# Moving a scale into the forget gates, and four 512-element operations to GpSimd, in a three-stage software pipeline

## The chip, the cores and the metric

The kernel runs on one core of a Trainium2 chip. A core has five engines that run side by side, each taking its own instructions strictly in order, and that wait for each other through semaphores: PE (TensorE, matrix products into PSUM), DVE (VectorE, elementwise), ACT (ScalarE, functions from tables), POOL (GpSimd, [...] the issuing of some DMAs) and SP (SyncE, the other DMAs). The metric is the device time of one execution in microseconds (us). Before the change it is 5087.27 us, the median of three runs (5086.96 to 5087.37).

## The reference, cut to what matters

The program is four layers on an image of 256x256 pixels with 128 channels. Layer 1 is the one touched here; its 128 channels are the real and imaginary parts of 64 complex ones. A complex spectrum A is taken from a 7x7 kernel, scaled to a bounded magnitude, and applied 16 times per pixel with a gate for each part:

```python
mag = jnp.sqrt(Ar ** 2 + Ai ** 2 + 1e-08)
scale = 0.95 * jax.nn.sigmoid(mag) / (mag + 1e-08)
Ar = Ar * scale
Ai = Ai * scale
...
def step(h_state, _):
    h_r, h_i = h_state
    Ah_r = Ar * h_r - Ai * h_i
    Ah_i = Ar * h_i + Ai * h_r
    return ((fg_r * Ah_r + inp_r, fg_i * Ah_i + inp_i), None)
```

The 16 steps multiply by the same 2x2 matrix per pixel and channel, M = [[fr Ar, -fr Ai], [fi Ai, fi Ar]]. The kernel therefore doesn't loop over the steps: with the trace t = (fr + fi) Ar and the determinant d = fr fi (Ar² + Ai²) it forms the sum of the first 16 powers of M as a polynomial by repeated squaring (squares of t and d, 2nd, 4th, 8th, 16th).

## The kernel before, in words

`recurrence` handles the image in NB = 64 blocks of four image rows. A block is a set of tiles of 128 partitions by 512 elements (called thin) or by 2x512 = 1024 (called wide), all float32. The work of a block is cut into about 75 small steps, each a one-line function named after what it makes. One hand-written tuple, `order`, lists (step, lag) pairs: iteration `it` runs each step for block `it - lag`, so three blocks are in work at once. Every step is pinned, so that each engine's instruction order is the order of this tuple restricted to the engine. The steps that matter below:

- lag 0: the products `zd`, `za`, `zf` (PE); `zaa`, which copies the spectrum out of PSUM into `ar`, and `a2`, its square (ACT); `m2`, the sum of the two squares (PE); `lm`, `mg`, `lb`, `iv`, `sg`, the functions that give the magnitude and its inverse (ACT); `f`, the two forget gates (ACT); `q`, then `s`, the scale, then `A`, which multiplies `ar` by the scale (DVE).
- lag 1: `A2`, the square of the scaled A (ACT), and `pa`, the sum of its two halves (PE); `ff` and `pf`, product and sum of the gates, `d_` (which reads `pa`), `t`, `D_` (DVE); the squarings `tq2`, `tq4`, `tq8`, `tq16`, `dn2`, `dn4`, `dn8` (ACT) between `tr2`, `u2`, `tr4`, `u4`, `tr8`, `u8` (DVE); the input path `zb`, `zi`, `bx` (PE), `xn`, `ig` (ACT), `p0`, `p1`, `qg`, `v` (DVE); `xa`, `y1` (DVE).
- lag 2: `y0`, `tr16`, `xb`, `be`, `e_`, `al` (DVE); `av` (PE); `yf`, `t1`, `yb` (DVE); `pox`, `po1`, `po2` (PE); `ev_`, `bn` (ACT). `ev_` also starts the DMA that writes the block (POOL's queue, L1044).

In the profile the DVE steps appear as L914 (two-operand, through `tt`) and L917 (scalar-and-two-operand, through `stt`), ACT steps as L54, its table loads as L889, PE steps as L60; a step is recognised by its tiles: the numbers are left out of names, so `tq2` to `tq16` are all `tq`, `tr2` to `tr16` `tr`, `u2` to `u8` `u`, `y0` and `y1` `y`. `t<-u,t` is `al`, `t<-t,g` is `e_`, `g<-t,u` is `xa`, `q<-q,ig` is `qg`.

PSUM is full: the products of tag "z" (`zd`, `za`, `zb`, `zf`, `zi`) share two buffers, those of tag "y" (`bx`, `av`, `po`) share one, and those of tag "s" (`m2`, `pa`) two of one bank each. So `av` can't begin until `v` has read `bx`, `pox` not until `yf` has read `av`, and the next `bx` not until `ev_` has read `po`.

## Time and profile before

| what | us |
|---|---|
| median of three runs | 5087.27 |
| span of the profiled execution | 5083.0 |
| the recurrence, first `zd` to last `ev_` | 1697.0 to 3219 |
| its steady part, one iteration per 23.31 us | 1734 to 3179 |
| PE, DVE, ACT busy in those 1445.0 us | 1406.31, 1444.89, 1392.10 |
| POOL busy there (62 DMA issues) | 33.11 |

The profile holds one execution, and its time is its span, 5083.0 us from the first to the last instruction; the 4.3 us up to the median of the runs lie around the span. [...] back to back, DVE starts a 512-element operation every 0.60 us and a 1024-element one every 1.135 us, though one lasts 0.69 and 1.22. The 62 iterations from 1734 to 3179 repeat to a hundredth of a microsecond.

### The profile page before, as it was taken

The page shows a single profiled execution, that of the slowest core. Times are in us where ns is not written, and L with a number is a line of the kernel's source. Part 1 is how long each engine was busy: PE and PEld are TensorE (multiplying, and loading weights), DVE is VectorE, ACT ScalarE, POOL GpSimd, SP SyncE. Part 2 cuts the span into 40 slices and gives each one's busy share as a digit, 9 for nine tenths or more (in the row PEclk, how much of TensorE's full clock was granted, in tenths as well). Part 3 has the DMA queues.
Part 4 walks back from the last instruction along what each step waited for, and adds up shares of the span by engine and source line. Part 5 has one row for each costly group of instructions (what it writes and reads, how often), then busy time and mean ns, then how long its engine had stood idle before and what let it go on. Part 6 is the DMA issues. An engine that isn't in the chain of part 4 may idle for free.

```text
span 5083.0 us, 78992 instructions
## 1 busy us (share of the span) xinstructions
PE 4951.9 (97%) x31563; PEld 2715.8 (53%) x31563; DVE 4100.4 (81%) x4797; ACT 3496.8 (69%) x4948; POOL 406.9 (8%) x592
## 2 busy tenths in 40 slices
PE   8999999999999899999999999899999999999999
PEld 2444555555555333333333333329999953359999
DVE  6666999999999799999999999775333537779886
ACT  6445888888888899999999999453333357762110
POOL 0331000000000000000000000240111010000000
PEclk9999999999999999999999999999999999999999
DMA  8894222222222222222222221688667778865432
GB/s 290 292 338 173 88 80 84 84 80 88 84 80 84 68 68 68 72 64 76 64 73 67 72 68 60 218 324 309 237 229 243 252 286 321 324 233 180 142 122 67
DMA packets 204463, 781.69 MB, mean 154 GB/s; under 512 B 56278, under 2 KB 59628, under 8 KB 154788
## 3 DMA queue, kind: packets, MB, share of 16 engines
q1 hardware_dynamic: 146638, 505.57, 29.8%
q0 software_dynamic: 56160, 270.64, 14.8%
q8 instruction: 252, 4.13, 0.3%
q14 instruction: 117, 0.96, 0.1%
q10 hardware_dynamic: 1296, 0.40, 0.0%
HBM read 505.18 MB, written 271.32 MB: 153 GB/s over the span
## 4 chain that ended last, share of the span: by engine, by line
PE 57%; DVE 29%; issue 5%; ACT 1%; POOL 0%; DMA 0%; POOLq 0%; DVEq 0%; SPq 0%; ACTq 0%
PE z L60 9%; PE m L60 7%; PE nd L60 7%; PE sc L60 5%; PE zc L60 5%; PE po L60 4%; DVE tr L917 3%; DVE t L914 3%; DVE y L914 3%; DVE p L914 3%; DVE yf L914 3%; PE ppq L60 3%; PE ppv L60 2%; PE px L60 2%; PE pe L60 2%
## 5 line engine op out<-in xcount | busy, mean ns | idle before, releaser
L576 DVE TENSOR_TENSOR e<-sc,bT 128x1024 f32<-128x1024 f32 x512 | 603.1, 1220 | 49.8 <-PE sc L60 48.9
L54 ACT ACTIVATE e<-e 128x1024 f32<-128x1024 f32 x512 | 540.4, 1055 | 61.5 <-DVE e L576 52.4
L1077 DVE TENSOR_TENSOR LR<-z,sg 128x512 f32<-128x512 f32 x256 | 268.4, 1049 | 363.0 <-ACT sg L54 363.0
L60 PE MATMUL m<-U,v 128*128 128x128 f32 x4608 | 514.8, 275 | 0.0
L60 PEld LDWEIGHTS m<-U,v 128*128 128x128 f32 x4608 | 514.6, 192 | 0.0
L60 PE MATMUL z<-wf,zt 128*128 128x128 f32 x4096 | 459.6, 276 | 1.4 <-DVE zn L1077 1.4
L60 PEld LDWEIGHTS z<-wf,zt 128*128 128x128 f32 x4096 | 459.4, 192 | 2.3 <-DVE zn L1077 2.2
L54 ACT ACTIVATE sg<-z 128x512 f32<-128x512 f32 x256 | 152.9, 597 | 307.7 <-PE z L60 307.7
L54 ACT ACTIVATE sq<-zs 128x1024 f32<-128x1024 f32 x192 | 202.4, 1054 | 192.1 <-DVE zs L385 156.1
L576 DVE TENSOR_TENSOR ks<-e 128x1024 f32<-128x1024 f32 x256 | 301.0, 1217 | 0.0
L60 PE MATMUL sc<-tq,tk 32*128 32x256 f32 x4096 | 297.0, 401 | 3.0 <-DVE e L576 2.1
L60 PEld LDWEIGHTS sc<-tq,tk 32*128 32x128 f32 x4096 | 186.4, 184 | 159.6 <-issue 96.3
L60 PE MATMUL nd<-e,tv 128*32 128x256 f32 x4096 | 271.0, 382 | 0.0
L54 ACT ACTIVATE dn<-dn 128x512 f32<-128x512 f32 x384 | 241.9, 630 | 13.0 <-DVE dn L576 2.3
L60 PE MATMUL av<-y,ident 128*128 128x512 f32 x384 | 192.9, 611 | 44.0 <-DVE y L914 44.0
L60 PE MATMUL po<-LR 128*128 128x256 f32 x1024 | 222.2, 380 | 6.9 <-DVE LR L1077 6.9
L1462 ACT COPY m4s<-m 128x512 f32<-128x512 f32 x32 | 18.7, 583 | 287.2 <-PE m L60 287.2
L60 PEld LDWEIGHTS po<-LR 128*128 128x128 f32 x1024 | 194.1, 190 | 34.2 <-DVE LR L1077 7.7
L60 PE MATMUL bx<-p,ident 128*128 128x512 f32 x384 | 192.4, 610 | 0.0
L54 ACT ACTIVATE o<-po 128x256 f32<-128x256 f32 x256 | 84.3, 381 | 145.3 <-issue 110.5
L60 PEld LDWEIGHTS nd<-e,tv 128*32 128x32 f32 x4096 | 120.1, 109 | 108.2 <-issue 42.1
L889 ACT ACT_TABLE_LOAD x132 | 169.4, 1283 | 1.5
(366 smaller groups left out, 10321.1 us busy)
## 6 DMA issues: line engine op xcount, KB each, us to landing
zt<-znT SPq DMA_DIRECT2D x128, 1024.0 KB
znT<-zn POOLq DMA_DIRECT2D x64, 1024.0 KB, 5.2
xin<-x2T SPq DMA_DIRECT2D x64, 1024.0 KB
xin<-in_x_dram SPq DMA_DIRECT2D x50, 1024.0 KB
xr<-x3T SPq DMA_DIRECT2D x46, 768.0 KB
xT<-xo POOLq DMA_DIRECT2D x32, 1024.0 KB, 9.3
xr<-xT SPq DMA_DIRECT2D x64, 512.0 KB
zn<-znT SPq DMA_DIRECT2D x64, 512.0 KB
```

Of the source, the lines that this page charges most:

```text
L54: return self.nc.scalar.activation(out, in_, func, bias=bias, scale=scale, **kw)
L60: return self.nc.tensor.matmul(out, lhsT, rhs, start=start, stop=stop)
L576: pin = lambda f: lambda *a, **k: tc.keep_in_program_order(f(*a, **k))
L889: pin(nc.scalar.preload_act_table_set(want))
L914: pin(V.tensor_tensor(out, a, b_, op))
L917: pin(V.scalar_tensor_tensor(out, a, k, b_, op0, op1))
L1077: pin = lambda f: lambda *a, **k: tc.keep_in_program_order(f(*a, **k))
L1462: nc.scalar.copy(m4, m[4])
```

## The change

The scale is no longer multiplied into A. Since A only ever enters as f times A, the two forget gates are multiplied by it instead (`fs_` in place of `A`, of the same size), the determinant reads the unscaled `m2`, and `A2` and `pa` go. `ff`, `u2` and `al` go from DVE to GpSimd, `tq4` from ACT to GpSimd, and some entries of `order` are moved. The DMA of `ev_` is pinned into the same order. `ar` gets a second buffer, `A` and `A2` vanish.

```diff
+            def gt(out, a, b_, op):
+                pin(nc.gpsimd.tensor_tensor(out, a, b_, op))
...
-            def zaa(d): act(wide(d, "ar"), d["za"].rearrange("p r i v -> p i r v"), AF.Copy)
-            def A(d):
-                sb = d["s"].rearrange("p (r v) -> p r v", v=N).unsqueeze(2).to_broadcast([P, 2, 2, N])
-                tt(rows(wide(d, "A", 2)), rows(d["ar"]), sb, MUL)
-            def A2(d): act(wide(d, "A2"), d["A"], AF.Square)
-            def pa(d): total(d, "pa", [[(self.ident, d["A2"][:, 0]), (self.ident, d["A2"][:, 1])]])
-            def ff(d): tt(thin(d, "ff"), d["f"][:, 0], d["f"][:, 1], MUL)
+            def zaa(d): act(wide(d, "ar", 2), d["za"].rearrange("p r i v -> p i r v"), AF.Copy)
+            def fs_(d): tt(d["f"], d["f"], both(d["s"]), MUL)
+            def ff(d): gt(thin(d, "ff"), d["f"][:, 0], d["f"][:, 1], MUL)
...
-            def t(d): tt(thin(d, "t", 2), d["fs"], d["A"][:, 0], MUL)
-            def d_(d): tt(thin(d, "d", 2), d["pa"][:, 0], d["ff"], MUL)
+            def t(d): tt(thin(d, "t", 2), d["fs"], d["ar"][:, 0], MUL)
+            def d_(d): tt(thin(d, "d", 2), d["m2"][:, 0], d["ff"], MUL)
...
-            def u2(d): tt(thin(d, "u2"), d["t"], d["tr2"], MUL)
-            def tq4(d): squared(d, "tq4", "tr2")
+            def u2(d): gt(thin(d, "u2"), d["t"], d["tr2"], MUL)
+            def tq4(d): gt(thin(d, "tq4"), d["tr2"], d["tr2"], MUL)
...
-            def al(d): tt(d["t"], d["u8"], d["t"], SUB)
-
-            def y0(d): tt(wide(d, "y0"), d["A"], both(d["v"][:, 0]), MUL)
-            def y1(d): tt(wide(d, "y1"), d["A"], both(d["v"][:, 1]), MUL)
+            def al(d): gt(d["t"], d["u8"], d["t"], SUB)
+
+            def y0(d): tt(wide(d, "y0"), d["ar"], both(d["v"][:, 0]), MUL)
+            def y1(d): tt(wide(d, "y1"), d["ar"], both(d["v"][:, 1]), MUL)
...
-                nc.gpsimd.dma_start(x2T[:, b * 1024:(b + 1) * 1024], d["x2"])
+                pin(nc.gpsimd.dma_start(x2T[:, b * 1024:(b + 1) * 1024], d["x2"]))
...
-                (zd, 0), (y0, 2), (tr16, 2), (za, 0), (xn, 1), (ff, 1), (A2, 1), (ab, 0), (pa, 1), (av, 2), (ae, 0),
+                (zd, 0), (y0, 2), (tr16, 2), (za, 0), (xn, 1), (ab, 0), (av, 2), (ae, 0),
                 (xb, 2), (d_, 1), (eD, 2), (pf, 1), (a2, 0), (al_, 0), (be, 2), (zaa, 0), (dn2, 1), (t, 1), (dn4, 1),
-                (m2, 0), (e_, 2), (lm, 0), (yf, 2), (zb, 1), (al, 2), (D_, 1), (t1, 2), (yb, 2), (pox, 2), (tq2, 1),
-                (po1, 2), (po2, 2), (mg, 0), (tr2, 1), (lb, 0), (lD, 1), (zf, 0), (p0, 1), (p1, 1), (iv, 0), (u2, 1),
-                (sg, 0), (tq4, 1), (ev_, 2), (f, 0), (q, 0), (tr4, 1), (s, 0), (dn8, 1), (zi, 1), (u4, 1), (A, 0),
-                (bx, 1), (tq8, 1), (ig, 1), (tr8, 1), (qg, 1), (bn, 2), (u8, 1), (tq16, 1), (v, 1), (xa, 1), (y1, 1),
+                (m2, 0), (e_, 2), (lm, 0), (al, 2), (yf, 2), (zb, 1), (D_, 1), (t1, 2), (yb, 2), (pox, 2), (tq2, 1),
+                (po1, 2), (po2, 2), (mg, 0), (tr2, 1), (lb, 0), (lD, 1), (zf, 0), (u2, 1), (tq4, 1), (p0, 1), (p1, 1), (iv, 0),
+                (sg, 0), (ev_, 2), (f, 0), (q, 0), (tr4, 1), (s, 0), (dn8, 1), (zi, 1), (u4, 1), (fs_, 0),
+                (bx, 1), (tq8, 1), (ig, 1), (tr8, 1), (qg, 1), (bn, 2), (u8, 1), (tq16, 1), (v, 1), (ff, 0), (xa, 1), (y1, 1),
```

On GpSimd the order per iteration becomes `al`, `u2`, `tq4`, the DMA of `ev_`, `ff`. On DVE it is that of before without `ff`, `u2` and `al`, with `fs_` where `A` was.

## The prediction

> **What bounds the kernel now.** I read the table of stages first, for the steady part of the recurrence alone (columns: stretch, its length, then busy time and instructions of PE, PEld, DVE, ACT, POOL, the clock, DMA share, GB/s):

> ```profile
> 1734.00:3179.00 1445.00, 1406.31 (x4713) 468.00 (x4712) 1444.89 (x1798) 1392.10 (x2047) 33.11 (x62) 1.00 0.22 68
> ```

> DVE works for 1444.89 of 1445.00 us. PE (97%) and ACT (96%) are close behind. So time leaves this stage only as fast as DVE work does, and only until the next limit. The timeline of DVE gives the iteration (start, duration):

> ```profile
> 2410.01 1.22 DVE L917 SCALAR_TENSOR_TENSOR v<-q,bx 128x1024 f32<-128x1024 f32 x1
> 2411.14 0.69 DVE L917 SCALAR_TENSOR_TENSOR g<-t,u 128x512 f32<-128x512 f32 x1
> 2411.74 2.36 DVE L914 TENSOR_TENSOR y<-A,v 128x1024 f32<-128x1024 f32 x2
> ...
> 2414.61 0.69 DVE L914 TENSOR_TENSOR ff<-f 128x512 f32<-128x512 f32 x1
> 2415.21 0.69 DVE L914 TENSOR_TENSOR g<-g,tr 128x512 f32<-128x512 f32 x1
> ...
> 2433.31 1.22 DVE L917 SCALAR_TENSOR_TENSOR v<-q,bx 128x1024 f32<-128x1024 f32 x1
> ```

> `v` to `v` is 23.30 us (23.31 over many). A 512-element step takes 0.60 from start to start, a 1024-element one 1.135: 18 x 0.60 + 11 x 1.135 = 23.29. No gap is left. The PE timeline of the same iteration shows the next limit:

> ```profile
> 2408.72 1.94 PE L60 MATMUL zd<-xf,gwd 128*64 128x512 f32 x8
> 2410.59 1.13 PE L60 MATMUL za<-ev,hs 14*128 14x512 f32 x4
> 2411.65 1.98 PE L60 MATMUL pa<-A,ident 128*128 128x512 f32 x4
> 2414.24 1.10 PE L60 MATMUL av<-y,ident 128*128 128x512 f32 x2 [0.61 <-DVE y L914]
> ...
> 2430.22 1.88 PE L60 MATMUL bx<-p,ident 128*128 128x512 f32 x4
> 2432.03 1.94 PE L60 MATMUL zd<-xf,gwd 128*64 128x512 f32 x8
> ```

> From `av` (2414.24) to the end of `bx` (2430.22 + 1.88 = 2432.10) PE runs without a gap, 17.86 us. Then `v` needs `bx`, and the next `av` needs `y0`, the fourth DVE operation from `v`: `v` at 2410.01 to `av` at 2414.24 is 4.23. This is a ring, `av` to `bx` on PE, then `v`, `xa`, `y1`, `y0` on DVE, and back to `av`; with 0.04 us between PE's end and `v` it can't turn faster than 17.86 + 0.04 + 4.23 = 22.13 us. Today `v` comes 1.2 us after `bx` (2432.10 against 2433.31), so the ring is slack by that much and nobody sees it.

> [...] GpSimd's zn runs beside DVE operations with a PSUM input (the rows of tile zn: count, shortest/median/longest ns):

> ```profile
> L1077 DVE TENSOR_TENSOR zn<-zs,pr x63: 1210/1214/1222, 3234.6 to 3429.4; 128x1024 f32<-128x1024 f32 x63
> L1175 POOL TENSOR_SCALAR zn<-zn,ln2in_w,ln2in_b x62: 1188/1190/1196, 3235.9 to 3427.0; 128x1024 f32<-128x1024 f32 x62
> ```

> Neither is stretched. [...] after 2.63 us without work four passes of `pa` took 3.25 us, after 1.32 us four of `po` took the usual 1.98.

> **The change part by part.**

> *Scale in the gates.* `A` (1024 elements, 1.135) becomes `fs_` (1024, 1.135): DVE unchanged. ACT loses `A2`, 0.94 from start to start; PE loses `pa`, 1.81. Neither bounds: nothing by themselves. Nor does the ring contain `pa`; it sits in the 4.23 us where PE waits for `y0` anyway. There PE now has `zd` and `za` alone, 2.93 us, and idles about 1.3: at the length of gap that left the clock whole, so I take no loss.

> *Three operations off DVE* (`ff`, `u2`, `al`): 3 x 0.60 = 1.80. DVE needs 21.50. ACT also loses `tq4` (0.52) and needs about 22.7 - 0.94 - 0.52 = 21.2, the 22.7 being 23.31 less its waits of some 0.6. So the ring, 22.13, is late next: the gain is cut from 1.80 to 1.18 per iteration.

> *Four operations on GpSimd.* No two-input operation of GpSimd is in the trace. [...] The nearest row, one input of 1024, is 1.19. [...]

> If only their length mattered: `al` starts when `e_` is done and `t1` needs it after `yf` and `D_`, 1.135 + 0.60 = 1.73 later. `u2` and `tq4` start after `tr2`, and `tr4` needs `tq4` after `p0`, `p1`, `q`, 3.4 later[...]. `ff` has until `d_` in the next iteration, some 8 us. The DMA of `ev_`, 0.53, sits between `tq4` and `ff`; nothing is late behind it, as `fs_` comes more than 2 us after `ev_`. `d_` and the two others add a wait each on DVE, none of them late.

> [...] `al` begins beside `yf` (reads `av` in PSUM), 0.2 after its start (the end of `e_` and 0.1 of signalling)[...]. `u2` and `tq4` begin beside `p0` and `p1` (read `zb` in PSUM), 2.27 long[...]. Both lie outside the ring's DVE part, where DVE has 22.13 - 21.50 = 0.63 to give[...]. `ff` is the open one. Its place in the list is behind `v`, but that orders it only among GpSimd's own; it may start once `fs_` is done, beside `tr8`, `qg`, `u8`, all with two SBUF inputs. From below 0 (it waits until `v`, which reads PSUM, and is hidden there)[...]. I take the lower end with an overhang onto `xa` of 0.15, because DVE's queue is full there and hands over from one instruction to the next with no gap (each starts 0.09 before the end of the last). Iteration: 22.13 + 0.15 = 22.3.

> *Sum.* 62 steady iterations x (23.31 - 22.3) = 62.6 us. At both ends `A2` and `pa` leave chains that are waited for (at the start `d` waits 4.79 us for `pa`, in the last iterations `pa` 2.63 us for A2); most of it goes into other waits, I take 2. Span 5083.0 - 65 = 5018; the runs lie 4.3 above: 5022.7.

> **The rivals.**
> 1. *`ff` gets the port in front of `qg`.* It asks while `tr8` runs, and `qg` asks later; that speaks for it, the dense queue against. [...] With the ends: 5084. Chance 0.18 (of it 0.04 faster, 0.12 level, 0.02 slower).
> 2. *The slower side: the port makes GpSimd's operations DVE's bill.* [...] For it: no run of before has such an operation[...]. Against: three of four start beside PSUM readers. Chance 0.26.
> 3. *The ring isn't one:* PE's 17.86 shrinks and DVE's 21.50 decides, 62 x 1.81 = 112, time 4973. Against it, PE's passes start every 0.45 us in that stretch without a wait to lose. Chance 0.04.

> **How the numbers follow.** Likeliest, 0.52: 5023, its own range 5010[...] to 5060 (iteration 22.9). The measurement tells 0.2%, 10 us, from no change. Faster: 0.52 + 0.04 + 0.04 = 0.60; same 0.12; slower 0.02 + 0.26 = 0.28. For 8 in 10 I leave out rival 3 and about half of rival 2: 5008 to 5125.

> **What would show it.** Right: `v` to `v` at 22.2 to 22.4 us; `v` waiting for `bx` on PE; PE idle 1.3 to 1.5 us before `av` at full clock; [...]`ff` ending beside `v`. Wrong: DVE durations above 0.69 and 1.22 for `D`, `q<-ex,az` or `q<-q,ig` (the port), GpSimd operations of 1.5 us and more, DVE waiting for POOL at `tr4` or `t1`, or a granted clock below 1.00 between 1734 and 3179.

## The result and the profile after

The changed kernel takes 5124.0 us (median of four runs, 5122.51 to 5127.5) against 5087.11 for the one before: 1.0074 times as long, with a 95% interval of 1.006 to 1.0088. It gives less work to DVE, ACT and PE and is 37 us slower. Its span is 5121.2 us, 38.2 above that of before.

The stage table of the changed kernel, for the stretch that was shown of the kernel before (same columns; the clock is the number third from the right):

```profile
1734.00:3179.00 1445.00, 1320.87 (x4346) 459.98 (x4344) 1366.54 (x1574) 1260.96 (x1871) 344.56 (x301) 0.93 0.22 68
```

DVE is no longer full: 1366.54 of 1445.00 us. PE and ACT are emptier as well. No engine bounds the stage, so a chain of waits must; and the clock, 1.00 before, is 0.93. The PE timeline of one iteration of the changed kernel:

```profile
2400.42 1.88 PE L60 MATMUL bx<-p,ident 128*128 128x512 f32 x4
2402.23 1.94 PE L60 MATMUL zd<-xf,gwd 128*64 128x512 f32 x8
2404.10 1.13 PE L60 MATMUL za<-ev,hs 14*128 14x512 f32 x4
2407.27 2.05 PE L60 MATMUL av<-y,ident 128*128 128x512 f32 x2 [2.04 <-DVE y L914]
2409.11 1.59 PE L60 MATMUL av<-y,negid 128*128 128x512 f32 x2
2410.54 1.88 PE L60 MATMUL av<-y,ident 128*128 128x512 f32 x4
2412.25 1.88 PE L60 MATMUL m<-a,ident 128*128 128x512 f32 x4
...
2424.32 1.88 PE L60 MATMUL bx<-p,ident 128*128 128x512 f32 x4
```

`pa` is gone from between `za` and `av`, and PE idles there for 2.04 us. Then `av` is slow: from its start to that of `m` it takes 4.98 us, before 3.51. The stage table in slices of 1 us shows why; `za` ended at 2405.23:

```profile
2405.00:2406.00 1.00, 0.23 (x2) 0.00 (x0) 1.00 (x2) 0.97 (x2) 0.00 (x0) 1.00 0.86 240
2406.00:2407.00 1.00, 0.00 (x0) 0.00 (x0) 1.00 (x1) 0.98 (x2) 0.00 (x0) 0.92 1.01 258
2407.00:2408.00 1.00, 0.73 (x1) 0.50 (x2) 0.97 (x3) 0.99 (x2) 0.00 (x0) 0.50 0.13 27
...
2410.00:2411.00 1.00, 1.00 (x4) 0.52 (x3) 1.00 (x3) 1.00 (x2) 0.00 (x0) 0.88 0.00 0
2411.00:2412.00 1.00, 1.00 (x4) 0.52 (x3) 0.45 (x1) 0.97 (x3) 0.47 (x1) 1.00 0.00 0
```

PE gets half its clock for 3.4 us (the shares of the slices at 2406 and 2410 put it from 2406.84 to 2410.24), once in every iteration. It begins while PE is still idle, 0.43 us before `av`, and `av` pays.

Why PE waits so long is in the timelines of DVE and POOL of the changed kernel:

```profile
2399.62 0.68 DVE L920 SCALAR_TENSOR_TENSOR tr<-dn,tq 128x512 f32<-128x512 f32 x1
2400.55 1.96 DVE L914 TENSOR_TENSOR q<-q,ig 128x1024 f32<-128x1024 f32 x1 [0.25 <-ACT ig L54]
2402.44 0.68 DVE L914 TENSOR_TENSOR u<-u,tr 128x512 f32<-128x512 f32 x1
2403.04 1.21 DVE L920 SCALAR_TENSOR_TENSOR v<-q,bx 128x1024 f32<-128x1024 f32 x1
```

```profile
2399.85 1.58 POOL L917 TENSOR_TENSOR ff<-f 128x512 f32<-128x512 f32 x1 [2.42 <-DVE f L914]
```

`ff` starts while `tr8` runs, lasts 1.58 us (1.28 in e6, where it runs beside `v`) and is finished at 2401.43. `qg` (`q<-q,ig`), which waited for `ig` until 2400.55, ends 1.08 us after `ff`, about the time that it takes from start to start by itself (1.135), and so lasts 1.96 instead of 1.22. This wait of a DVE operation for one on GpSimd, counted into its duration, is what the recorded texts and this document call the port; the trace shows the times, not what the two engines share. `v` therefore starts 0.74 us after `bx` ended (2402.30), where nothing else was in its way.

The ring of the prediction closes on these rows: `av` to the end of `bx` 18.93 (2407.27 to 2426.20), then 0.74 to `v`, then 4.23 to the next `av`, together 23.90 us, against an iteration of 23.31 before. 62 x 0.59 = 36.6 of the 38.2 us.

### The profile page after: what moved, and what is told of

Its sections match the earlier page's. It is cut to its first block, busy times and chain, and to the rows that moved or that the text cites. A ratio compares the mean times of both kernels' runs of the same rounds, so it can differ in the third digit from the quotient of the medians.

```text
span 5121.2 us, 78615 instructions
## 1 busy us (share of the span) xinstructions
PE 4898.3 (96%) x31307; PEld 2719.2 (53%) x31307; DVE 4053.6 (79%) x4605; ACT 3394.5 (66%) x4820; POOL 737.3 (14%) x848
## 4 chain that ended last, share of the span: by engine, by line
PE 73%; DVE 9%; ACT 5%; issue 4%; POOL 0%; DMA 0%; POOLq 0%; DVEq 0%; ACTq 0%; SPq 0%
PE m L60 9%; PE po L60 9%; PE z L60 9%; PE nd L60 7%; PE av L60 6%; PE sc L60 5%; PE zc L60 5%; DVE y L914 3%; PE ppq L60 3%; DVE q L914 2%; PE ppv L60 2%; PE px L60 2%; PE zf L60 2%; PE pe L60 2%; PE ppg L60 2%
## 5 line engine op out<-in xcount | busy, mean ns | idle before, releaser
L60 PE MATMUL m<-U,v 128*128 128x128 f32 x4608 | 514.8, 275 | 0.0
L60 PEld LDWEIGHTS m<-U,v 128*128 128x128 f32 x4608 | 514.6, 192 | 0.0
L60 PE MATMUL z<-wf,zt 128*128 128x128 f32 x4096 | 461.0, 276 | 1.4 <-DVE zn L1076 1.4
L60 PEld LDWEIGHTS z<-wf,zt 128*128 128x128 f32 x4096 | 460.8, 193 | 2.3 <-DVE zn L1076 2.2
L60 PE MATMUL av<-y,ident 128*128 128x512 f32 x384 | 251.8, 772 | 137.5 <-DVE y L914 137.5
L60 PE MATMUL sc<-tq,tk 32*128 32x256 f32 x4096 | 297.1, 401 | 2.8 <-DVE e L576 2.0
L60 PEld LDWEIGHTS sc<-tq,tk 32*128 32x128 f32 x4096 | 186.5, 184 | 159.6 <-issue 96.3
L60 PE MATMUL nd<-e,tv 128*32 128x256 f32 x4096 | 271.0, 382 | 0.0
L60 PEld LDWEIGHTS av<-y,ident 128*128 128x128 f32 x384 | 90.0, 254 | 268.4 <-issue 268.4
L60 PE MATMUL po<-LR 128*128 128x256 f32 x1024 | 222.2, 380 | 6.9 <-DVE LR L1076 6.9
L60 PEld LDWEIGHTS po<-LR 128*128 128x128 f32 x1024 | 194.1, 190 | 34.2 <-DVE LR L1076 7.7
L685 POOL DMA_DIRECT2D x1T<-x x64 | 34.1, 533 | 1213.8 <-DVE x L576 1181.7
L60 PE MATMUL bx<-p,ident 128*128 128x512 f32 x384 | 193.3, 612 | 0.0
```

What stands on the lines that cost most here:

```text
L60: return self.nc.tensor.matmul(out, lhsT, rhs, start=start, stop=stop)
L685: nc.gpsimd.dma_start(x1T[:, (rp - 1) * 512:(rp + 1) * 512], x1)
```

## The experiments

Two suspects follow: the port (`ff` in front of `qg`) and the clock (PE's idle time where `pa` stood). Does the clock drop only because the port lengthens the idle time, or by itself? And is the scale in the gates, which looked free, the loss?

**e1_ff_vector** takes the port's conflict away:

```diff
-            def ff(d): gt(thin(d, "ff"), d["f"][:, 0], d["f"][:, 1], MUL)
+            def ff(d): tt(thin(d, "ff"), d["f"][:, 0], d["f"][:, 1], MUL)
...
-                (zd, 0), (y0, 2), (tr16, 2), (za, 0), (xn, 1), (ab, 0), (av, 2), (ae, 0),
+                (zd, 0), (y0, 2), (tr16, 2), (za, 0), (xn, 1), (ff, 1), (ab, 0), (av, 2), (ae, 0),
```

(and the entry of `ff` behind `v` goes.)

> The changed kernel with ff back on VectorE at its old place; u2, tq4 and al stay on GpSimd. Theory (port first, clock behind it: ff in front of qg makes v 0.7 us late, which lengthens TensorE's idle time ahead of av to 2.04 us, at which the clock drops): qg 1.22 us instead of 1.97, the idle time ahead of av about 1.3 us, the clock whole, v to v 22.2 to 22.4 us, time 5020 to 5035. Rival (the clock drops at 1.3 us too, since pa no longer fills the gap): clock in the steady part about 0.93, av still slowed, v to v 23.0 to 23.3, time 5070 to 5090.

5075.82 us, ratio 0.9979 (0.9972 to 0.9987). `qg` is back at 1.23 us and the idle time at 1.35, as the theory had it. But the clock is 0.94, and the rival is right. The PE timeline of e1 in an iteration with the drop:

```profile
2409.66 1.68 PE L60 MATMUL av<-y,ident 128*128 128x512 f32 x2 [1.35 <-DVE y L914]
2411.13 1.91 PE L60 MATMUL av<-y,negid 128*128 128x512 f32 x2
2412.84 2.19 PE L60 MATMUL av<-y,ident 128*128 128x512 f32 x4
```

From `v` to `v`, e1's iterations are of two kinds: 22.40 us, about every fourth or fifth, and 23.1 to 23.4. In 47 of 60 `yf` had to wait for `av`; those are the slow ones. The idle time doesn't tell them apart. It is 1.35 us in both kinds, and 2.00 only in the iteration after a fast one. The stage table of e1 has two idle times of 1.35 us, each in a window of 3.41 us, that is, between two neighbouring points of the grid on which the traces show the clock change (last section), and each followed by the next window:

```profile
2406.64:2410.05 3.41, 2.06 (x9) 0.60 (x6) 3.41 (x6) 2.70 (x4) 0.00 (x0) 1.00 0.54 148
2410.05:2413.46 3.41, 3.41 (x5) 1.35 (x4) 3.41 (x7) 3.40 (x5) 0.00 (x0) 0.50 0.03 6
...
2454.42:2457.84 3.42, 2.07 (x7) 0.68 (x4) 3.42 (x5) 3.36 (x5) 0.00 (x0) 1.00 0.55 153
2457.84:2461.25 3.41, 3.41 (x9) 1.52 (x8) 3.41 (x7) 3.41 (x5) 0.00 (x0) 1.00 0.00 0
```

PE was busy for 2.06 and 2.07 us, and the clock dropped behind the first only. The first idle time began 1.67 us into its window, the second 0.74.

**e2_pe_filler** takes the idle time away and leaves the port:

```diff
+            def fill(d): total(d, "fill", [[(self.ident, d["xf"][:, :512]), (self.ident, d["xf"][:, 512:])]])
...
-                (zd, 0), (y0, 2), (tr16, 2), (za, 0), (xn, 1), (ab, 0), (av, 2), (ae, 0),
+                (zd, 0), (y0, 2), (tr16, 2), (za, 0), (xn, 1), (ab, 0), (fill, 1), (av, 2), (ae, 0),
```

> The changed kernel with two matmuls of 128x512 whose result nobody reads where pa stood (the work of pa, added to what the kernel computes). Theory (the clock's drop is worth 1.1 us per iteration, the port the rest): clock 1.00 in the steady part, the idle time ahead of av 0.2 to 0.3 us, qg still 1.97 us, v to v about 22.8 us, time 5050 to 5065: adding work makes it faster. Rival (av is late for another reason, the slower passes are a symptom): v to v stays at 23.9, time 5124 or above.

5064.76 us, 0.9959 (0.9945 to 0.9973). As the theory had it, two matmuls that nobody reads make the changed kernel 59 us faster. Its stage table (stretch to 3150):

```profile
1734.00:3150.00 1416.00, 1374.65 (x4692) 471.61 (x4690) 1413.86 (x1604) 1287.47 (x1910) 352.22 (x308) 1.00 0.22 69
```

The clock is whole, and DVE is busy throughout; part of that is `qg`, which now lasts 2.29 us, waiting for `ff`. The iteration is 22.97, a little above the 22.8 expected; the idle time 0.69, not 0.2 to 0.3.

**e3_scale_only** is the other half of the change: the kernel before with `fs_` for `A`, without `A2` and `pa`, and with nothing on GpSimd.

```diff
-            def A2(d): act(wide(d, "A2"), d["A"], AF.Square)
-            def pa(d): total(d, "pa", [[(self.ident, d["A2"][:, 0]), (self.ident, d["A2"][:, 1])]])
+            def fs_(d): tt(d["f"], d["f"], both(d["s"]), MUL)
...
-            def d_(d): tt(thin(d, "d", 2), d["pa"][:, 0], d["ff"], MUL)
+            def d_(d): tt(thin(d, "d", 2), d["m2"][:, 0], d["ff"], MUL)
```

> The kernel before with the scale in the gates only: fs_ for A, A2 and pa gone, all else on VectorE and ScalarE and in the old order; nothing on GpSimd. Theory (without pa TensorE idles some 2.4 us ahead of av and the clock drops there): av about 1.1 to 1.5 us longer, of which 0.9 is covered by what VectorE has to do before yf; v to v 23.5 to 23.9, time 5100 to 5125, slower than before with less work. Rival (VectorE has the same work and nothing else bounds): 23.31, time 5085 to 5089.

5122.78 us, 1.0071 (1.0054 to 1.0088), again the theory. Leaving out a squaring and two matmuls, with DVE's work as it was, costs the whole loss. The stage table of e3:

```profile
1734.00:3150.00 1416.00, 1294.08 (x4263) 448.53 (x4261) 1383.62 (x1717) 1262.24 (x1893) 31.41 (x59) 0.93 0.21 68
```

**e4_zb_early** tries to use the gap for work that is needed:

```diff
-                (zd, 0), (y0, 2), (tr16, 2), (za, 0), (xn, 1), (ab, 0), (av, 2), (ae, 0),
+                (zd, 0), (y0, 2), (tr16, 2), (za, 0), (xn, 1), (ab, 0), (zb, 1), (av, 2), (ae, 0),
```

> The changed kernel with zb one stage earlier in the order, ahead of av, so that its 1.06 us lie in TensorE's gap and not between av and bx. Theory (gap too long, ring too long): idle time ahead of av about 1 us, clock whole, the ring 22.83 - 1.06 = 21.8 and VectorE with the stretched qg about 22.4 to 22.6; time 5030 to 5045. Rival (clock drops all the same): av slowed, v to v about 22.9 to 23.3, time 5060 to 5090.

5123.23 us, 1.0072 (1.0055 to 1.0088): a miss. The PE timeline of e4:

```profile
2408.43 1.13 PE L60 MATMUL zb<-ev,hs 14*128 14x512 f32 x4 [0.31 <-ACT az L54]
2411.23 2.08 PE L60 MATMUL av<-y,ident 128*128 128x512 f32 x2 [1.67 <-DVE y L914]
```

`zb` fills part of the gap, but it leaves the stretch from `av` to `bx`, so that `bx` ends sooner (2405.20) while DVE, with `qg` at 2.29 us here too, comes to `v` only at 2407.10: 1.67 us of idle time remain behind `zb`. The clock drops in every iteration (0.93).

**e5_ff_vector_fill** is e1 with one matmul of filler in the place of e2's two:

```diff
+            def fill(d): total(d, "fill", [[(self.ident, d["xf"][:, :512])]])
```

> The changed kernel with ff back on VectorE (as e1_ff_vector) and one matmul of 128x512 that nobody reads where pa stood (added work). In e1 the iterations in which the clock stayed whole took 22.40 us and the others 23.43. Theory (TensorE's idle time ahead of av sets the clock, and nothing else was late there): idle time 0.4 to 0.5 us, clock 1.00, every iteration 22.4 us, time 5029 to 5036. Rival (the 22.40 were a recovery from the slow ones, with buffers filled ahead): 22.6 to 22.9, time 5040 to 5060.

5043.52 us, 0.9921 (0.9904 to 0.9937). Neither theory nor rival holds throughout: iterations of 22.4 us, as the theory had it, and still some of 23.41; `yf` waited for `av` in 16 of 61. The 22.40 of e1 were no recovery, then, but the idle time, mostly 0.95 us in the timeline and not the 0.45 that I had worked out, is still enough to lose the clock now and then (0.98).

**e6_ff_held_fill** keeps `ff` on GpSimd, but holds it back with a copy of one column of `q`, which waits for `qg`, and has e5's filler:

```diff
+            def hold(d): pin(nc.gpsimd.tensor_copy(tp.tile([P, 1], F32, name="hold", tag="hold", bufs=1), d["q"][:, 0, 0:1]))
...
-                (bx, 1), (tq8, 1), (ig, 1), (tr8, 1), (qg, 1), (bn, 2), (u8, 1), (tq16, 1), (v, 1), (ff, 0), (xa, 1), (y1, 1),
+                (bx, 1), (tq8, 1), (ig, 1), (tr8, 1), (qg, 1), (bn, 2), (u8, 1), (tq16, 1), (v, 1), (hold, 1), (ff, 0), (xa, 1), (y1, 1),
```

> The changed kernel with the same one unread matmul (added work), and on GpSimd ahead of ff a copy of one column of q that waits for qg, so that ff can only start beside u8 and v. Theory [...]: qg 1.22 us, ff about 1.3 us, at most 0.3 us of wait on u8 or xa, clock 1.00, iteration 22.2 to 22.5, time 5022 to 5037. Rival (ff costs VectorE about 0.7 us wherever it runs): u8, v or xa stretched by that, iteration 22.7 to 23.0, time 5050 to 5066.

5002.77 us, 0.9838 (0.9821 to 0.9854), and 22.00 us per iteration, both better than I expected. DVE and then POOL in e6:

```profile
2415.62 0.68 DVE L914 TENSOR_TENSOR u<-u,tr 128x512 f32<-128x512 f32 x1
2416.22 1.21 DVE L920 SCALAR_TENSOR_TENSOR v<-q,bx 128x1024 f32<-128x1024 f32 x1
2417.35 0.78 DVE L920 SCALAR_TENSOR_TENSOR g<-t,u 128x512 f32<-128x512 f32 x1
```

```profile
2415.83 0.51 POOL L977 COPY hold<-q 128x1 f32<-128x1 f32 x1 [4.63 <-DVE q L914]
2416.30 1.28 POOL L917 TENSOR_TENSOR ff<-f 128x512 f32<-128x512 f32 x1
```

`ff` runs beside `v`, which reads `bx` from PSUM: neither is stretched (1.28 and 1.21). Only `xa`, with two inputs in SBUF, is 0.1 longer (0.78; 0.68 in the changed kernel).

**e7_moves_only** leaves A, `A2`, `pa` and `ff` as they were before, and moves `u2`, `tq4` and `al` to GpSimd in the new order:

```diff
-            def u2(d): tt(thin(d, "u2"), d["t"], d["tr2"], MUL)
-            def tq4(d): squared(d, "tq4", "tr2")
+            def u2(d): gt(thin(d, "u2"), d["t"], d["tr2"], MUL)
+            def tq4(d): gt(thin(d, "tq4"), d["tr2"], d["tr2"], MUL)
...
-            def al(d): tt(d["t"], d["u8"], d["t"], SUB)
+            def al(d): gt(d["t"], d["u8"], d["t"], SUB)
```

> The kernel before with u2, tq4 and al on GpSimd in the new order, and A, A2, pa and ff as they were. Theory (the moves are the gain, the scale in the gates is the loss through the gap that pa filled): clock 1.00, TensorE with pa is the bound at about 22.6, time 5040 to 5050: faster than both kernels. Rival (moving work to GpSimd is the loss): 23.3 or more, time 5087 or above.

5028.54 us, 0.9889 (0.9872 to 0.9905): faster than both kernels. At 22.38 us per iteration it is DVE that bounds it (1413.41 of 1416.00 us), not PE as I had written; PE idles for no more than 0.1 us ahead of `av`.

**e8_ff_held** is the corner that was missing, the changed kernel with e6's copy ahead of `ff` and no filler.

> The changed kernel with ff held back until qg is done (the one-column copy of e6_ff_held_fill), and no filler: the missing corner beside the changed kernel (neither), e2_pe_filler (filler alone) and e6_ff_held_fill (both, 22.00 us). Theory (TensorE's idle time ahead of av is 0.56 + 0.9 = about 1.4 us, at which the clock of e1_ff_vector dropped in three iterations of four): qg 1.22 us, clock about 0.94, iterations of 22.0 and of 23.0, on average 22.7 to 23.1, time 5045 to 5075. Rival (the port was the whole loss and the idle time only matters when it is above 2 us): clock 1.00, 22.0 throughout, time about 5003.

5074.98 us, 0.9977 (0.9968 to 0.9987), with the clock at 0.94: the theory, at its upper end (iterations of 21.97 and 23.48 us, 23.15 on average). PE's timeline in e8:

```profile
2408.36 1.48 PE L60 MATMUL av<-y,ident 128*128 128x512 f32 x2 [1.41 <-DVE y L914]
```

With it the two suspects stand apart (mean from `v` to `v`, us):

| | nothing where `pa` stood | filler |
|---|---|---|
| `ff` free to start | 23.90 (changed kernel) | 22.97 (e2, two matmuls) |
| `ff` held until `qg` is done | 23.15 (e8) | 22.00 (e6, one matmul) |

The clock is worth 0.93 to 1.15 us per iteration, the port 0.75 to 0.97. These are differences between four kernels, not fixed prices: in e8 the clock drops in three iterations of four, in the changed kernel in every one. Either alone would have eaten most of what the moves brought; the two together ate more.

**e9_moves_ff_held** puts the pieces together without filler: e7, with `ff` on GpSimd and held as in e6.

> e7_moves_only (A, A2 and pa kept, u2, tq4, al on GpSimd) with ff on GpSimd too, held back until qg is done. Nothing left out and nothing added but the copy of one column. Theory (VectorE then needs 21.9, and TensorE with pa 22.2, which turns the ring): 22.1 to 22.3 us, clock 1.00, time 5008 to 5022. Rival (VectorE isn't what bounds e7): 22.4 as in e7, time 5028.

5007.62 us, 0.9845 (0.9829 to 0.9862). Its iteration is 22.05 us, and the clock is 1.00, with `pa` doing useful work where e6 has a filler. Now it is PE that has no idle time (1340.00 us busy of 1340.00 from 1760 to 3100; DVE 1337.89). Its interval overlaps that of e6. A is scaled as before, and nothing is added but the copy.

## Why the prediction was wrong

- *Bound by DVE, ring next at 22.13:* DVE is right, the ring's size is not. With the clock whole and the port free the iteration is 22.00, and DVE still bounds it (e6: 1337.90 us busy of 1340.00 from 1760 to 3100). PE's stretch from `av` to `bx`, which I took as gapless and fixed at 17.86, ran 0.40 us faster in the changed kernel from `m2` to the end of `bx` (13.95 against 14.35), and as fast in e6; why isn't shown. So much of rival 3 was true.
- *"There PE now has `zd` and `za` alone, 2.93 us, and idles about 1.3: at the length of gap that left the clock whole, so I take no loss."* This is the step that failed. The gap was sized rightly (1.35 us in e1, 1.40 in e8, where the port is out of the way), but not its cost, which I put at nothing. I took that from one gap of 1.32 us, where full speed followed. In e1 and e8 1.35 to 1.41 us lost the clock in 34 of 47 cases each, and the 2.04 us of the changed kernel lose it in every iteration: `av` takes 4.98 us instead of 3.51. My one example was luck: that gap began 0.70 us into its window of the clock, and in e1 and e8 a place as early as this lost nothing either. The failed step alone accounts for e3: no work added, 37 us slower.
- *The price of `ff`:* I put it at 0.15 on `xa`, an estimate, arguing that DVE's dense queue would come first. That the two engines hold each other up at all was assumed: the rows of `zn` show them side by side, neither stretched. The runs show far more than 0.15: `ff`, started beside `tr8`, is through before `qg`, and `v` is 0.70 us later than `bx` would have let it start. In the changed kernel DVE isn't dense there (`qg` waits 0.25 us for `ig`). In e2 it is, `ff` comes first all the same, and `qg` is stretched by 1.07 (2.29 against 1.22). Rival 1 named exactly this, and put it at 5084, since it too left the clock out.
- *Length of GpSimd's operations:* the prediction's rested on no trace. Measured: 1.27 to 1.28 for two different inputs (`al`, `u2`), 1.04 for `tq4`, which reads one tile twice. `q` (`q<-ex,az`), behind `u2` and `tq4`, is 0.10 longer (1.32 against 1.22), `D` behind `al` 0.17 in e6 (0.85 against 0.68). So rival 2 (each a bill for DVE) falls: in e7 three of them together leave the gain.
- *"Scale in the gates ... nothing by themselves":* wrong in sign. It is the part that costs, by taking PE work out of a place where it kept the clock up (0.93 in e3, 1.00 before).

Against the ring's 22.13, the changed kernel has 1.47 us more for `av` at half clock, 0.40 less from `m2` to `bx` and 0.70 more for `v` behind the port: 23.90. The range of 5008 to 5125 holds the measured 5124.0 only through the share of rival 2, whose mechanism did not come true; that is luck.

With the clock whole and the port free the iteration would have gained 1.31 us (23.31 to 22.00, e6, filler and copy included); clock and port together cost 1.90 (22.00 to 23.90), which leaves the loss of 0.59 that was measured.

## What to carry to other kernels

Before removing work from an engine that isn't the bound, look at what that work separated: here the kernel whose PE idled for 2.04 us in each turn was slower than the same one with two more matmuls there (23.90 us against 22.97, e2), so read the clock along with the idle time, iteration by iteration. Look at what DVE runs beside an operation moved to GpSimd: `ff` made `qg`, with two inputs in SBUF, 0.74 to 1.07 us longer (changed kernel, e2), and `v`, which reads PSUM, not at all (1.21, e6). Its place in the list of steps didn't put it beside `v`: in the changed kernel `ff` started 3.19 us earlier (2399.85 against 2403.04), 0.15 after its input `f` was finished. Where a change joins two edits, run each alone; here one was worth 57 us (e7) and the other cost 37 (e3). Both together, with `ff` still on DVE, took 10 us off (e1); `ff` on GpSimd then cost another 48.
